# Splitting the gathers of four of the last tiles between GpSimd and two hardware queues

## The chip, the cores and the metric

The kernel runs on one core of one Trainium2 chip. The metric is the device time in microseconds (us) of an execution. An NT of 1574 tiles of 128 edges, some 41,600 instructions, make up one execution.

## The reference, cut to what matters

A relational graph convolution with a residual, over 12,500 nodes of 256 features, 212,500 edges sorted by their target node, and 8 types of edges:

```
h   = max(layernorm(x), 0)
hx  = einsum('ni,rio->rno', h, weight)          # 8 relations
msg = hx[edge_type, src]                        # one row of 256 for each edge
agg = segment_sum(msg, dst, 12500)
out = x + agg * sqrt(0.5) + h_bias + (h @ loop_weight) * sqrt(0.5)
```

The kernel turns the order round: it first sums the normalized rows h[src] by (target, type), and multiplies the sums by the 8 weights afterwards.

## The kernel before, in words

**Tiles and units.** The edges are cut into 1574 tiles (NT) of 128 edges. Two tiles (PAIR) make a unit. For each tile the 128 rows h[src] of 1 KB stand in SBUF, one row a partition, in half of a buffer `msg`; there are 33 such buffers of two tiles. h32 is the normalized table in DRAM.

**Sums.** `edge_sums(t)` multiplies the tile's rows by a one-hot matrix (`oh`, made on VectorE) of its targets and types: four fp32 matmuls on TensorE (L1105), into a PSUM bank `ps`. `add_sums` (L1141, VectorE) adds a unit's sums to the accumulator `acc`, a ring over 768 nodes. When all edges of a group of 128 nodes are summed, 16 products with the weights and 2 with the loop's weight follow (L1321, 32 and 4 matmuls as the profile counts them), VectorE adds x and the bias (L1307, L1338), and SP's queue stores the rows (L1350, and L1341 and L1344 for the last groups). The products of one group are spread between the sums of later tiles. The last group's products can only come after the last tile. Where the ring has turned, `wrap` (L1287) moves its overlap before the next group's products.

**Two ways for a tile's rows.** Most tiles are gathered by one indirect DMA that GpSimd issues (`gather`, L1009). `goal(t)` says how far the gathers run ahead of the sums: 24 tiles in the middle, and `max(8, (NT - t) // 5)` near the end, so 8 tiles in the last 40. Each gather is also held until the last whole unit before its place in the program has been summed ("no faster than the sums"). Its landing is counted on one of 68 semaphores, on which the tile's first matmul waits.

Some tiles (t % 54 in 25 or 53, up to 16 tiles before the end, and also NT - 15 = 1559 and NT - 1 = 1573) are not gathered at all. `begin_fetch(t)` is called 40 tiles (FAR) ahead; it gives the tile its buffer, if it has none yet, and puts five parts (`SOURCES`) on two lists, one for SP's queue (28 + 32 rows) and one for ScalarE's (24 + 20 + 24 rows). From 8 tiles (HOLD) after that, `fetch(n)` takes up to n entries a tile from each list. An entry is either a load of a part's offsets into registers (`load_sources`, L1030) or the DMA of one row (`fetch_row`, L1038). The queues' engines work their instructions off in order and run ahead of the sums as far as buffers and counters permit. SP's queue also carries the loads of x and h (L1258) and the stores of the output; a store waits on VectorE. ScalarE's queue carries little else.

**Counters.** The rows of a fetched tile are counted on one of COUNTERS semaphores, 16 for each row; TensorE waits for the count (L1101) ahead of the tile's matmuls. A semaphore is used again by the fetched tile COUNTERS places later in the list, whose first row waits until the earlier tile is summed.

The fetched tiles near the end are 1483, 1511, 1537, 1559 and 1573.

Of the kernel before, what the change touches and what calls it, by code (L numbers as in the profile page):

```python
# [20 lines left out]
SP = mybir.EngineType.SP  # L21
ACT = mybir.EngineType.Activation

P = 128
# [16 lines left out]
NEAR = 8  # L41
# [21 lines left out]
SINGLE = 54  # L63
PLACED = (25, 53)
CLOSING = 15
SOONER = 64
FETCH = 4
SOURCES = ((0, 28, "SP"), (28, 24, "ACT"), (52, 20, "ACT"), (72, 32, "SP"), (104, 24, "ACT"))
HOLD = 8
FAR = 40  # L70
STORE = 44
COUNTERS = 4
LANDINGS = 68


# [186 lines left out]
def kernel(  # L262
# [11 lines left out]
    nc = tc.nc  # L274
# [10 lines left out]
    NT = plan.NT  # L285
# [46 lines left out]
    def reach_of(t):  # L332
        b, half, row = place_of(t)
        return REACH[half] if b < NB - 1 or NB > 1 and row < NARROWED else (0, WIN)

    def place_of(t):
        u, i = divmod(t, PAIR)
        half = 0 if PAIR * u + 1 == NT else PAIR - 1 - i
        b, row = row_of(u)
        return b, half, row  # L340


    with ExitStack() as main:
# [32 lines left out]
        single, fetches, stores = {}, {SP: [], ACT: []}, []  # L376
        counters = [tc.alloc_semaphore(f"rows{i}") for i in range(COUNTERS)]
        fetched, summed = {}, {}
        landings = [tc.alloc_semaphore(f"landed{i}") for i in range(LANDINGS)]
        landed = {}  # L380
        state = {"h32": None}
# [482 lines left out]
        for d in range(0, N, XG * P):  # L864
            k = min(XG, (N - d) // P)
# [96 lines left out]
        def room(t):  # L962

            both = msgs.tile([P, PAIR, D], F32, name="msg")
            for i in range(PAIR):
                msg[t + i] = both[:, i, :]

        def in_turn(t):

            return t % SINGLE in PLACED  # L970

        def filled(t):

            _, half, _ = place_of(t)
            return min(P, EU - half * P) if t // PAIR == NU - 1 and NB > 1 else P

        def single_rows(t):

            return ((t in (NT - 1, NT - CLOSING) or in_turn(t) and t + 2 * NEAR < NT)
                    and state["h32"] is not None and t // QUAD * QUAD >= state["h32"] + LATE + AHEAD)  # L980

        def begin_fetch(t):

            if t not in msg:
                room(t - t % PAIR)
            fetched[t] = len(fetched)
            for r, n, name in SOURCES:
                engine = SP if name == "SP" else ACT
                fetches[engine].append((
                    done["tile"] + HOLD,  # L990
                    lambda r=r, n=n, engine=engine: load_sources(t, r, n, engine)))

        def gather(t):
            if t % PAIR == 0 and t not in msg:
                room(t)
            if t % QUAD:
                kind[t] = kind[t - 1]
            else:
                kind[t] = "h" if state["h32"] is not None and t >= state["h32"] + LATE else "x"
            table = {"h": h32, "x": x}[kind[t]]  # L1000
            b, i, u = place_of(t)
            if single_rows(t) and t not in fetched and t - done["tile"] >= FAR:
                begin_fetch(t)
            if t in fetched:
                return
            at = i * P + u
            n = filled(t)
            of = direct[:, i : i + 1] if t < PAIR else gidx[b][:, at : at + 1]
            i = nc.gpsimd.indirect_dma_start(  # L1009
                out=msg[t][:n], out_offset=None, in_=table[:, :],  # L1010
                in_offset=bass.IndirectOffsetOnAxis(ap=of[:n], axis=0))
            if kind[t] == "h":
                n = landed[t] = len(landed)
                i.then_inc(landings[n % LANDINGS], 16)
                tc.no_tile_sem_insts.add(i.ins.name)
                tc.add_to_no_dep_group(f"landed{t}", i.ins)
            if "unit" in latest:
                tc.add_manual_dep(
                    i.ins, latest["unit"], SYNC_DEP, reason="no faster than the sums")
# [7 lines left out]
        def load_sources(t, r0, count, engine):  # L1027

            b, _, u = place_of(t)
            _, vals = nc.values_load_multi_w_load_instructions(  # L1030
                single[b][u : u + 1, r0 : r0 + count], engines=[engine],
                min_val=0, max_val=(N - 1) * D * 4,
                skip_runtime_bounds_check_because="clamped to the table where they are computed")
            queue = {SP: nc.sync, ACT: nc.scalar}[engine]
            k = fetched[t]

            def fetch_row(i, v):
                j = queue.dma_start(  # L1038
                    msg[t][r0 + i : r0 + i + 1, :].bitcast(U8), h32_bytes[:, bass.ds(v, D * 4)])
                j.then_inc(counters[k % COUNTERS], 16)  # L1040
                tc.no_tile_sem_insts.add(j.ins.name)
                tc.add_to_no_dep_group(f"rows{t}", j.ins)
                if i == 0 and k >= COUNTERS:
                    tc.add_manual_dep(
                        j.ins, summed[k - COUNTERS], SYNC_DEP, reason="counter is at rest")

            for i, v in reversed(list(enumerate(vals))):
                fetches[engine].insert(0, (0, lambda i=i, v=v: fetch_row(i, v)))

        def fetch(n):  # L1050
            for list_ in fetches.values():
                for _ in range(n):
                    if list_ and list_[0][0] <= done["tile"]:
                        list_.pop(0)[1]()
# [29 lines left out]
        def edge_sums(t):  # L1084
            m, o = msg.pop(t), oh.pop(t)
            if t % PAIR == 0:
                bank = banks[t // PAIR % BANKS]
                sums["ps"] = bank[:, : KC * R * WIN].rearrange("p (c k) -> p c k", c=KC)
            ps = sums["ps"]
            i = t % PAIR  # L1090
            b, half, _ = place_of(t)
            first, width = (R * n for n in reach_of(t))
            end = t == NT - 1 or i == PAIR - 1
            free = added.get(t // PAIR - BANKS)
            if i == 0 and free is not None and latest["pe"] is not None:
                tc.add_manual_dep(latest["pe"], free.name, SYNC_DEP, reason="bank is free")
            if i == 0 and latest["pe"] is not None:
                tc.add_manual_dep(latest["pe"], made[t], SYNC_DEP, reason="one-hots are made")
            if t in fetched:
                k = fetched[t]  # L1100
                j = nc.tensor.wait_ge(counters[k % COUNTERS], 16 * P * (k // COUNTERS + 1))  # L1101
                tc.declare_fence(j.ins, group=f"rows{t}")
            used = filled(t)
            for c in range(KC):
                j = nc.tensor.matmul(  # L1105
                    ps[:, c, first : first + width], m[:used, c * P : (c + 1) * P], o[:used, :width],
                    start=(i == 0 and c == 0), stop=(end and c == KC - 1), skip_group_check=True)
                if t in landed and c == 0:
                    n = landed[t]
                    j.wait_op(landings[n % LANDINGS], 16 * (n // LANDINGS + 1), "sem-ge")  # L1110
                    tc.declare_no_dep(
                        j.ins, group=f"landed{t}", reason="waits for the landing by count")
                    tc.declare_fence(j.ins, group=f"landed{t}")
                else:
                    in_run("sums", j, end and (c == KC - 1 or t == NT - 1))
            latest["pe"] = j.ins
            if end:
                latest["unit"] = j.ins.name
            if t in fetched:
                summed[fetched[t]] = j.ins.name  # L1120
            return ps
# [270 lines left out]
        with tc.manual_schedule():  # L1392
# [21 lines left out]
            for t in range(PAIR):  # L1414
                gather(t)
# [72 lines left out]
            def blocks_ahead(t):  # L1488
                for b in range(1, NB):
                    if b == NB - 1 > 1 and t == PAIR * (RAW + P * (b - 1)) - PREP - SOONER:  # L1490
                        fill_in(b)
# [51 lines left out]
            for t in range(NT):  # L1543
# [5 lines left out]
                    gathered += 1  # L1549
                while t < NT - HELD and stores and stores[0][0] <= t:  # L1550
                    stores.pop(0)[1]()
                fetch(FETCH)
                blocks_ahead(t)
                credit = min(0.0, credit) + SHARE - (0.52 if t % PAIR else 0.0)
                for f in after:
# [27 lines left out]
                if t % (PAIR * REGS) == 0 and t // PAIR + REGS < NU:  # L1583
                    load_offsets(t // PAIR + REGS)
                ps = edge_sums(t)
                while late and late[0][0] <= t:
                    late.pop(0)[1]()
                    credit -= 0.83
                advance(t)
                while writes and credit > 0:  # L1590
                    _, cost, f = writes.pop(0)
# [83 lines left out]
```

## Time and profile before

| what | value |
| --- | --- |
| median of 3 runs | 1936.13 us |
| the three runs | 1936.13, 1936.15, 1932.9 us |
| the profiled execution, its own time | 1932.58 us |
| its span, first to last instruction | 1930.9 us |
| mean granted TensorE clock | 0.960 |
| busy: TensorE matmul, weight load | 1684.4 us (87%), 1441.3 us (75%) |
| busy: VectorE, ScalarE, GpSimd | 1325.9 us (69%), 132.0 us (7%), 1445.7 us (75%) |
| DMA, mean rate | 144 GB/s |

All numbers but the first two rows come from the one profiled execution. PE is TensorE's matmuls, PEld its weight loads, DVE is VectorE, POOL GpSimd; SPq and ACTq are the two hardware queues' issuing instructions, which are not counted as busy. A row of the chain has its start, its length and what it was, in us; a row of the timeline has start, length, engine, line, operation, the tile written and read, the count, and in brackets the engine's idle time before it with what ended it. L1009 is line 1009 of the kernel before.

### The profile page before, as it was taken

To read this page: it belongs to the slowest core of one execution; us is meant where nothing else is said; L and a number is where in the kernel's file an instruction comes from. 1 tells how busy PE (TensorE), PEld (TensorE's weight loads), DVE (VectorE), ACT (ScalarE), POOL (GpSimd) and SP (SyncE) were. 2 spreads that over 40 slices of the span, in tenths; PEclk is the share of its full clock that TensorE was granted. 3 is DMA by queue.
4 is the path that set the end of the run, shared out by engine and by line. 5 is a ranking of instruction groups with operands and counts; after the bars stand their busy time and mean duration, and the time that the engine had idled before them with its cause. 6 is when DMAs were issued, how large, how long until landed. Compare 5 with 4: busy or idle time off the path is not lost.

```text
span 1930.9 us, 41561 instructions
## 1 busy us (share of the span) xinstructions
PE 1684.4 (87%) x10136; PEld 1441.3 (75%) x10136; DVE 1325.9 (69%) x3353; ACT 132.0 (7%) x286; POOL 1445.7 (75%) x1546
## 2 busy tenths in 40 slices
PE   2367999999889999989888989898989888999998
PEld 2356889899778777777777777777777777777887
DVE  7888768976567965658766656776566885665653
ACT  6964000000000000000000000000000000000000
POOL 7777777777777777777777777777777777777774
PEclk9568999999999999999999999999999999999999
DMA  9974455445544444454444454444445444444443
GB/s 322 382 222 146 121 141 142 142 132 141 145 126 140 123 131 138 126 144 130 132 131 121 136 139 131 130 130 132 131 128 142 122 130 132 132 127 132 128 109 88
DMA packets 159057, 278.88 MB, mean 144 GB/s; under 512 B 35819, under 2 KB 110168, under 8 KB 158808
## 3 DMA queue, kind: packets, MB, share of 16 engines
q0 software_dynamic: 72960, 199.33, 36.3%
q1 hardware_dynamic: 77000, 73.08, 12.3%
q10 hardware_dynamic: 8848, 3.78, 1.0%
q8 instruction: 80, 1.31, 0.3%
q14 instruction: 169, 1.38, 0.2%
HBM read 250.45 MB, written 25.60 MB: 143 GB/s over the span
## 4 chain that ended last, share of the span: by engine, by line
PE 31%; POOL 27%; DMA 20%; issue 11%; DVE 7%; ACT 3%; DVEq 0%; SPq 0%; POOLq 0%; ACTq 0%
POOL msg L1009 27%; DMA msg<-h,gidx 19%; PE po L1321 16%; PE ps L1105 15%; ACT msg L931 1%; DVE acc L1141 1%; DVE stats L887 1%; DMA xt<-in_x_dram 1%; DVE oh L1066 1%; DVE moves L478 1%; ACT xt L931 1%; DVE acc L1183 1%; PE pt L1165 1%; ACT acc L1154 0%; DVE fixed L480 0%
## 5 line engine op out<-in xcount | busy, mean ns | idle before, releaser
L1009 POOL DMA_INDIRECT msg<-h,gidx x1432 | 1360.2, 950 | 439.1 <-issue 375.9
L1105 PEld LDWEIGHTS ps<-oh,msg 128*128 128x128 f32 x6296 | 915.7, 196 | 384.7 <-DMA msg<-h,gidx 261.9
L1105 PE MATMUL ps<-oh,msg 128*128 128x136 f32 (+1 forms) x6296 | 998.9, 288 | 197.6 <-DMA msg<-h,gidx 131.5
L1321 PE MATMUL po<-w,acc 128*128 128x256 f32 (+1 forms) x3136 | 881.5, 386 | 4.2 <-DVE acc L1141 3.0
L1141 DVE TENSOR_TENSOR acc<-acc,ps 128x352 f32 x788 | 406.5, 516 | 363.0 <-PE ps L1105 351.3
L1321 PEld LDWEIGHTS po<-w,acc 128*128 128x128 f32 (+1 forms) x3136 | 515.3, 192 | 42.0 <-issue 11.3
L1183 DVE SCALAR_TENSOR_TENSOR acc<-types,pt 128x256 f32<-128x256 bf16 x720 | 258.9, 412 | 76.0 <-PE pt L1165 65.3
L1066 DVE TENSOR_TENSOR oh<-fixed,cols 128x544 f32<-128x544 f32 x394 | 281.4, 714 | 0.0
L1321 PE MATMUL po<-wl,self_t 128*128 128x256 f32 (+1 forms) x392 | 111.8, 409 | 5.4 <-DVE self_t L1170 4.6
L1009 POOL DMA_INDIRECT msg<-in_x_dram,gidx x86 | 81.5, 948 | 26.2 <-issue 23.5
L1321 PEld LDWEIGHTS po<-wl,self_t 128*128 128x128 f32 (+1 forms) x392 | 71.2, 203 | 13.5 <-DVE self_t L1170 5.9
L1307 DVE TENSOR_TENSOR xr<-xr,po 128x256 f32<-128x256 f32 (+1 forms) x98 | 40.5, 413 | 19.1 <-PE po L1321 19.0
L1338 DVE TENSOR_TENSOR xr<-xr,po 128x256 f32<-128x256 f32 (+1 forms) x98 | 41.2, 421 | 10.4 <-PE po L1321 7.0
L478 DVE TENSOR_SCALAR moves<-fixed 128x336 int32<-128x336 int32 (+1 forms) x96 | 44.6, 465 | 5.2 <-DVE acc L1141 3.7
L931 ACT ACTIVATE msg<-msg,shift,rstd 128x256 f32<-128x256 f32 x88 | 44.8, 587 | 6.9 <-DVE stats L895 4.5
L480 DVE COPY_PREDICATED fixed<-moves,fixed 128x335 int32<-128x335 int32 (+7 forms) x96 | 41.6, 433 | 3.3
L1237 DVE CAST types<-pt 128x512 bf16<-128x512 f32 x23 | 15.9, 690 | 40.0 <-PE pt L1233 39.1
L1170 DVE COPY self_t<-pt 128x256 f32<-128x256 f32 (+1 forms) x98 | 40.6, 414 | 2.2 <-PE pt L1165 2.2
L1165 PE MATMUL pt<-ident,hr 128*128 128x128 f32 (+1 forms) x196 | 38.3, 278 | 2.9 <-DMA hr<-h 1.5
L931 ACT ACTIVATE xt<-xt,shift,rstd 128x256 f32<-128x256 f32 x66 | 33.7, 587 | 9.8 <-DVE shift L928 9.8
L1221 DVE TENSOR_TENSOR of<-pt,line 22x512 bf16<-22x512 f32 x23 | 15.7, 682 | 20.4 <-PE pt L1214 20.2
L1165 PEld LDWEIGHTS pt<-ident,hr 128*128 128x128 f32 (+1 forms) x196 | 25.3, 149 | 5.3 <-DMA hr<-h 1.8
(179 smaller groups left out, 373.8 us busy)
## 6 DMA issues: line engine op xcount, KB each, us to landing
msg<-h ACTq DMA_DIRECT2D x3672, 1.0 KB
msg<-h SPq DMA_DIRECT2D x3240, 1.0 KB
msg<-h,gidx POOLq DMA_INDIRECT x1432, 5.1
hr<-h SPq DMA_DIRECT2D x23, 512.0 KB
xr<-in_x_dram SPq DMA_DIRECT2D x23, 512.0 KB
out_dram<-xr SPq DMA_DIRECT2D x22, 512.0 KB
xt<-in_x_dram SPq DMA_DIRECT2D x16, 512.0 KB
h<-xt SPq DMA_DIRECT2D x16, 512.0 KB
```

Of the source, the lines that this page charges most:

```text
L478: nc.vector.tensor_single_scalar(m, packed[:, :n], 1 << (bit + k), op=ALU.bitwise_and)
L480: nc.vector.copy_predicated(packed[:, : n - (1 << k)], m[:, 1 << k :], packed[:, 1 << k : n])
L931: nc.scalar.activation(row, row, AF.Relu, bias=shift[:n, j : j + 1], scale=rstd[:n, j : j + 1])
L1009: i = nc.gpsimd.indirect_dma_start(out=msg[t][:n], out_offset=None, in_=table[:, :], in_offset=bass.IndirectOffsetOnAxis(ap=of[:n], axis=0))
L1066: j = nc.vector.tensor_tensor(o[:, k : k + v, :i, :width], iota_f[:, :width].unsqueeze(1).unsqueeze(1).to_broadcast([P, v, i, width]), of. ...
L1105: j = nc.tensor.matmul(ps[:, c, first : first + width], m[:used, c * P : (c + 1) * P], o[:used, :width], start=(i == 0 and c == 0), stop=( ...
L1141: i = nc.vector.tensor_tensor(a, a, ps[:, c], op=ALU.add)
L1165: in_run("turns", nc.tensor.transpose(pst[:, c, :n], rows_[:n, c * P : (c + 1) * P], ident[:n, :n]), c == KC - 1)
L1170: nc.vector.tensor_copy(got["self", g][:, :, :n], pst[:, :, :n])
L1183: i = nc.vector.scalar_tensor_tensor(acc[:, :, r, s0 : s0 + n], of, float(r + 1), pst[:, :, :n], op0=ALU.is_equal, op1=ALU.mult)
L1321: i = nc.tensor.matmul(got["out", g][:n], lhs, rhs, start=(r == R and c == 0), stop=(r == R - 1 and c == KC - 1))
L1338: nc.vector.tensor_add(rows_[:n, k, :], rows_[:n, k, :], got["out", g][:n])
```

## The change

Four more of the last tiles are treated in both ways at once. `SPLIT` gives, by their distance from NT, how many of their 128 rows GpSimd still gathers, and which rows the two queues fetch one by one:

| tile | GpSimd | SP | ScalarE's queue |
| --- | --- | --- | --- |
| 1565 (NT - 9) | 124 | 4 | 0 |
| 1567 (NT - 7) | 96 | 16 | 16 |
| 1569 (NT - 5) | 92 | 16 | 20 |
| 1571 (NT - 3) | 64 | 32 | 32 |

TensorE waits for both counts at these tiles: for the gather's landing and for the rows' counter. The counters become eight, and each keeps the sum of the rows counted on it so far, as the tiles now differ in their numbers. In the last 40 tiles `fetch` takes up to 8 entries a tile from each list, not 4. The pairs 1564 to 1570 get their buffers 40 tiles ahead, with the fetched rows.

```
+SPLIT = {
+    9: (124, ((124, 4, "SP"),)),
+    7: (96, ((96, 16, "SP"), (112, 16, "ACT"))),
+    5: (92, ((92, 16, "SP"), (108, 20, "ACT"))),
+    3: (64, ((64, 32, "SP"), (96, 32, "ACT"))),
+}
...
-COUNTERS = 4
+COUNTERS = 8
...
+        counted = [0] * COUNTERS
...
         def single_rows(t):
-            return ((t in (NT - 1, NT - CLOSING) or in_turn(t) and t + 2 * NEAR < NT)
+            return ((t in (NT - 1, NT - CLOSING) or NT - t in SPLIT or in_turn(t) and t + 2 * NEAR < NT)
...
         def begin_fetch(t):
-            for r, n, name in SOURCES:
+            for r, n, name in SPLIT.get(NT - t, (0, SOURCES))[1]:
...
         def gather(t):
-            if t in fetched:
-                return
             at = i * P + u
             n = filled(t)
+            if t in fetched:
+                n = SPLIT.get(NT - t, (0, SOURCES))[0]
+            if not n:
+                return
...
         def edge_sums(t):
             if t in fetched:
-                k = fetched[t]
-                j = nc.tensor.wait_ge(counters[k % COUNTERS], 16 * P * (k // COUNTERS + 1))
+                k = fetched[t] % COUNTERS
+                counted[k] += 16 * sum(n for _, n, _ in SPLIT.get(NT - t, (0, SOURCES))[1])
+                j = nc.tensor.wait_ge(counters[k], counted[k])
...
-                fetch(FETCH)
+                fetch(FETCH if t < NT - FAR else 2 * FETCH)
```

## The prediction

> **What bounds the kernel now.** I read the page first (the chain's shares, the costliest group), then the chain of waits piece by piece through the last 90 us, then the queues' own issues in time, then single rows of TensorE and GpSimd. Tile numbers come from counting back along both engines: the last gather is tile 1572 and a gather is 1.25 us (0.95 busy, 0.30 between), so the gather at 1885.85 us is tile 1550's; four fp32 matmuls on L1105 are one tile's sums.
>
> ```profile
> POOL msg L1009 27%; DMA msg<-h,gidx 19%; PE po L1321 16%; PE ps L1105 15%; ACT msg L931 1%; DVE acc L1141 1%; DVE stats L887 1%; DMA xt<-in_x_dram 1%; DVE oh L1066 1%; DVE moves L478 1%; ACT xt L931 1%; DVE acc L1183 1%; PE pt L1165 1%; ACT acc L1154 0%; DVE fixed L480 0%
> L1009 POOL DMA_INDIRECT msg<-h,gidx x1432 | 1360.2, 950 | 439.1 <-issue 375.9
> ```
>
> GpSimd's gathers set the pace of the whole span, and the time in which a gather's rows are on their way (19%) is the second share. The end looks otherwise, in the chain's pieces (start, length, what):
>
> ```profile
> 1845.83 6.46 DMA msg<-h,gidx
> 1852.29 0.04 issue
> 1852.33 3.66 PE ps L1105 x16
> ...
> 1885.85 2.74 DMA msg<-h,gidx
> 1888.58 0.04 issue
> 1888.63 0.73 PE ps L1105 x4
> ...
> 1900.85 2.76 DMA msg<-h,gidx
> ...
> 1905.51 1.56 PE po L1321 x6
> ...
> 1917.95 7.19 PE po L1321 x32
> ```
>
> Two things are to be seen. The last wait for a gather on this chain ends at 1903.6, 2.76 us after 1900.85: tile 1563. All four tiles whose gathers the change shortens (1565, 1567, 1569, 1571) come after it, and from 1905.51 on TensorE works without waiting for any gather. And a gather took 6.46 us to land at 1845.83, 2.74 and 2.76 at 1885.85 and 1900.85. What differs is seen in the issues of the two queues (start, length of the stretch, count):
>
> ```profile
> 1774.23 26.71 SPq L1038 DMA_DIRECT2D msg<-h  x66
> ...
> 1803.53 17.06 SPq L1038 DMA_DIRECT2D msg<-h  x46
> 1829.49 0.41 SPq L1350 DMA_DIRECT2D out_dram<-xr  x1
> 1830.00 29.14 SPq L1038 DMA_DIRECT2D msg<-h  x74
> 1839.80 26.18 ACTq L1038 DMA_DIRECT2D msg<-h  x68
> L1030 ACTq TENSOR_LOAD <-single x17: 1536/1791/2713, 1700.1 to 1855.9; - x17
> L1030 SPq TENSOR_LOAD <-single x11: 1829/2124/2226, 1702.2 to 1846.6; - x11
> ```
>
> At 1845 both queues fetch single rows; the last row of tile 1573 is issued at 1859.1 on SP and at 1866.0 on ScalarE's queue, and after that gathers land in 2.7 us. More of it, from the chain earlier on, and from one wait that TensorE's row shows (tile 1488, gathered at 1810.81, awaited until 1818.03, so 7.2 us):
>
> ```profile
> 482.79 12.25 DMA msg<-h,gidx
> ...
> 1780.78 5.21 DMA msg<-h,gidx
> 1794.54 5.83 DMA msg<-h,gidx
> 1810.81 0.95 POOL L1009 DMA_INDIRECT msg<-h,gidx  x1 [0.30 <-issue]
> 1818.03 0.73 PE L1105 MATMUL ps<-oh,msg 128*128 128x136 f32 x4 [0.61 <-DMA msg<-h,gidx]
> ```
>
> With both queues at it from 1774 to 1820 the landing grows: 5.2, 5.8, 7.2 us. Then SP stands still for 8.9 us (1820.6 to 1829.5, the output store waits), and at 1845.8 it is 6.5. So fetched rows delay gathers, more the longer both queues run, and the last 40 us are the one stretch that is free of them. The change puts 136 more rows there.
>
> ```profile
> q10 hardware_dynamic: 8848, 3.78, 1.0%
> msg<-h ACTq DMA_DIRECT2D x3672, 1.0 KB
> ```
>
> ScalarE's queue moves 3672 rows of 1 KB in at most 8848 packets, about two for a row (the row and its completion): a row isn't spread over the 16 DMA engines. That one engine gets them all is not in these rows. [...]
>
> **The change part by part.**
>
> *Shorter gathers.* 4 + 32 + 36 + 64 = 136 rows leave GpSimd. In proportion that is 136/128 of 0.95 us, 1.0 us; at a fixed price of an instruction it is 0. Nothing shorter than 128 rows is in the trace, so 0 to 1.0. Either way it is hidden:
>
> ```profile
> 1903.35 0.95 POOL L1009 DMA_INDIRECT msg<-h,gidx  x1 [0.30 <-issue]
> 1912.10 0.95 POOL L1009 DMA_INDIRECT msg<-h,gidx  x1 [0.30 <-issue]
> 1908.67 0.59 PE L1105 MATMUL ps<-oh,msg 128*128 128x104 f32 x4
> 1914.80 2.71 PE L1105 MATMUL ps<-oh,msg 128*128 128x104 f32 x20
> L1101 PEldq EVENT_SEMAPHORE  x54: 51/51/51, 264.0 to 1914.9; - x54
> ```
>
> Tile 1565 lands about 1906.1 and is used at 1908.67; tile 1572 lands at 1914.85 and its matmuls, thirteenth of the last 20, come about 1.3 us later. I take 0.
>
> *Four more counter waits on TensorE*, 51 ns each, 0.2 us, on the queue that loads weights ahead. Between 0 and 0.2 I take 0.1.
>
> *Eight counters for four.* The first row of a fetched tile waits until the tile k places earlier in the list is summed. With four, tile 1573 would now wait for 1565, which is summed at 1908.67, too late; with eight it waits for tile 1483, ninety tiles earlier, of which GpSimd gathers 86 at 1.25 us: some 107 us before 1916.7. 0, and 0 for the earlier ones, which now wait for a sum further back.
>
> *Rows on ScalarE's queue.* 16 + 20 + 32 = 68 rows and 3 loads of offsets, ahead of tile 1573's 68 rows and 3 loads. The same set took 26.2 us plus its first load, 28 us, so tile 1573's last row goes out at 1866 + 28 = 1894 instead of 1866.
>
> *Rows on SP.* 4 + 16 + 16 + 32 = 68 rows and 4 loads. From tile 1534 on up to eight entries a tile are put on a queue, so the output store at 1829.49 now has behind it not 46 of tile 1559's 60 rows but all of them, tile 1565's four, and two loads: 18 rows at 0.32 us (17.06 less one load, over 46) and 2 loads of 2.2 are 10.2 us from 1820.6. The idle 8.9 us are filled and the store goes at 1830.8, 1.3 us later; nothing waits for it. Then 124 rows and 4 loads, 40 + 9 us, end at 1880 instead of 1859. Tile 1573 is summed from 1916.7: 22 us to spare on the slower queue.
>
> *What these rows do to the gathers.* Both queues now run unbroken from 1774 to 1880, then one until 1894. No row has the landing at 1885.85 (tile 1550, on the chain) under this load. Below: 2.74, if one queue alone does no harm, or 6.46, the value after 16 us of both. Above: 12.25, the value that the early part shows. From 7.2 at 1811 with the growth of 2.0 us in 30 us it would be about 11.8 at 1880; it then falls while ScalarE's queue is alone. I take 8. That is 5.3 us later than 2.74. TensorE takes some back:
>
> ```profile
> 1902.41 0.73 PE L1105 MATMUL ps<-oh,msg 128*128 128x136 f32 x4 [0.30 <-DMA msg<-h,gidx]
> 1903.65 0.69 PE L1105 MATMUL ps<-oh,msg 128*128 128x104 f32 x4 [0.51 <-DMA msg<-h,gidx]
> 1880.97 1.50 PE L1105 MATMUL ps<-oh,msg 128*128 128x104 f32 x12
> 1883.34 0.95 POOL L1009 DMA_INDIRECT msg<-h,gidx  x1 [0.30 <-issue]
> ```
>
> After 1888.63 it idles 0.30 + 0.51 = 0.81 us before the ring's wrap on VectorE ends and the next products start at 1905.51; afterwards only the last group's hand-over is idle, which moves along. So 5.3 - 0.8 = 4.5 us reach the end. A second effect adds: a gather is also held behind the sums of nine tiles before it. Tile 1548's (1883.34) waits for tile 1539's sums (first of the twelve matmuls from 1880.97, done 1881.55): 1.8 us to spare. TensorE has no idle time between 1852.33 and 1878, so a lateness of about 2 us from longer landings at 1852 arrives there whole and holds GpSimd by some 0.2 us, which no later gather makes up; at 3 us it would be 1.2. I take 0.4.
>
> *Sum:* 0 + 0.1 + 0 + 4.5 + 0.4 = 5.0 us. The profiled execution took 1932.58 us (span 1930.9), so 1937.6 against it. It is 3.6 us below the median of the runs shown, two of which are at 1936.1 and one at 1932.9; against the median it is 1936.13 + 5.0 = 1941.
>
> **The rivals.**
>
> *The landings recover in time.* Below 7.4 us at 1885.85 (2.74 + 0.81 + 3.9) less than 3.9 us reach the end, 0.2%, about what a measurement of this kernel can tell from no change. 6.46 gives 2.9 us: 1939. For it speaks that SP fills its rows with loads of 2.1 us, one for every 16 rows; against it that 7.2 was reached before the pause that now goes.
>
> *Rows and gathers don't collide there* (rows spread, or the growth had another cause): then TensorE's own work decides from 1905.51, and the time is 1936.2, not slower. It decides if the landing at 1885.85 stays under 3.6 us. Against it stand 6.46 and 2.74 on the two sides of the last fetched row.
>
> *GpSimd is the bound to the end*, and 136 rows less bring up to 1.0 us: 1935. Against it: 1.3 us to spare at tile 1572. More than 1.0 us isn't in it, so faster by over 0.2% needs the spread of the runs as well.
>
> *An uneven gather lands late.* 124 and 92 rows don't divide into 16 equal shares. If such a gather landed over 2.6 us later (tile 1565, 1908.67 - 1906.1) TensorE would stall at it; twice 2.7 us of landing would cost 0.1 us. [...]
>
> *The rows come too late for tile 1573*: it needs a pitch near twice 0.32 us. 1945 or more.
>
> **How the numbers follow.** Forecast (4 us and more) 0.57, late rows 0.03: slower 0.60. Recovery in time 0.24, no collision 0.09: the same 0.33. Faster 0.07, GpSimd's rows with a low run. Range: from the lower group of runs with little added (1932.6 + 1.4 = 1934) to a landing of 12 us and a GpSimd hold of 3 (1936.1 + 8.5 + 3 = 1948). The forecast's own range is 1937 to 1948.
>
> **What would show it.** Right: rows of L1038 on ScalarE's queue until about 1894 and on SP until 1880, no pause before the store on L1350; landings of 6 us and more on the chain between 1866 and 1885; longer waits on L1105 for gathers there; GpSimd's gaps over 0.30 us around tile 1548. The last stretch from 1905.51 to the end of the last group's products at 1925.14 keeps its 19.6 us. Wrong: landings near 2.8 us at 1885 with rows still being issued, or a gap before tile 1565's, 1569's or 1573's sums.

## The result, and the profile after

The changed kernel takes 1939.76 us (median of 8 runs, 1938.61 to 1942.82), the kernel before 1933.42 us (8 runs, 1931.02 to 1936.15): a ratio of 1.0032, 95% interval 1.0021 to 1.0043, so 6.3 us slower. All runs named e, f and h below were timed while the chip ran even the kernel before in 2387 to 2414 us, at a granted clock of 0.88 to 0.90 instead of 0.96, so every ratio is taken against the kernel before as timed beside that run. The profiled execution took 1940.04 us with a span of 1938.3 us, 7.4 us more than the one before. The lines of the changed kernel are shifted: the gather is L1018, the row fetch L1047, the sums L1115, their counter wait L1111, the products L1331, the wrap L1297.

The chain of the changed kernel, its last 75 us (start, length, what):

```profile
1867.02 9.98 DMA msg<-h,gidx
1877.00 0.04 issue
1877.04 1.18 PE ps L1115 x8
...
1891.18 0.08 issue
1891.26 5.75 DMA msg<-h,gidx
1897.01 0.04 issue
1897.05 0.73 PE ps L1115 x4
...
1912.76 1.56 PE po L1331 x6
...
1925.19 7.19 PE po L1331 x32
```

A gather took 9.98 us to land at 1867.02; in the kernel before, the last row had gone out by then (1866.0). The last gather on the chain is the same tile's as in the prediction's argument, 1550 (the 22nd from the end, the last one counted): it begins at 1891.26 instead of 1885.85 and lands in 5.75 us instead of 2.74. From 1897.05 no gather is waited for. The products after the wrap begin 7.25 us later than before (1912.76 against 1905.51), the last group's 7.24 us later (1925.19 against 1917.95): the tail itself is unchanged, it only starts late.

The queues' issues in time:

```profile
1804.14 23.93 SPq L1047 DMA_DIRECT2D msg<-h  x64
1830.13 0.41 SPq L1360 DMA_DIRECT2D out_dram<-xr  x1
1830.72 49.60 SPq L1047 DMA_DIRECT2D msg<-h  x124
1760.05 135.62 ACTq L1047 DMA_DIRECT2D msg<-h  x324
```

SP puts out all 60 rows of tile 1559 and four more ahead of the store, without the pause, and ends at 1880.3; ScalarE's queue ends at 1895.7.

GpSimd's gathers with a gap over 0.35 us, and the four short ones (1908.77, 1911.64, 1914.13, 1916.88) with the last:

```profile
1870.49 0.94 POOL L1018 DMA_INDIRECT msg<-h,gidx  x1 [1.27 <-PE pt L1175]
...
1875.59 0.94 POOL L1018 DMA_INDIRECT msg<-h,gidx  x1 [0.40 <-PE ps L1115]
...
1880.89 0.94 POOL L1018 DMA_INDIRECT msg<-h,gidx  x1 [0.61 <-PE ps L1115]
...
1885.26 0.94 POOL L1018 DMA_INDIRECT msg<-h,gidx  x1 [2.17 <-PE ps L1115]
...
1888.76 0.95 POOL L1018 DMA_INDIRECT msg<-h,gidx  x1 [1.31 <-PE ps L1115]
...
1908.77 1.30 POOL L1018 DMA_INDIRECT msg<-h,gidx  x1 [0.30 <-issue]
...
1911.64 0.92 POOL L1018 DMA_INDIRECT msg<-h,gidx  x1 [0.30 <-issue]
...
1914.13 1.19 POOL L1018 DMA_INDIRECT msg<-h,gidx  x1 [0.30 <-issue]
...
1916.88 0.91 POOL L1018 DMA_INDIRECT msg<-h,gidx  x1 [0.31 <-issue]
1918.09 0.95 POOL L1018 DMA_INDIRECT msg<-h,gidx  x1 [0.30 <-issue]
```

Before, none of the gaps in this stretch was over 0.31 us. Over that pace the five add 0.97 + 0.10 + 0.31 + 1.87 + 1.01 = 4.3 us, each ended by TensorE: GpSimd was held behind the sums. The rest of the 5.4 us by which tile 1550's gather begins late was there before any of the added rows went out. The gather that is 80th from the end, in the profile before and in this one:

```profile
1813.31 0.95 POOL L1009 DMA_INDIRECT msg<-h,gidx  x1 [0.30 <-issue]
...
1814.46 0.95 POOL L1018 DMA_INDIRECT msg<-h,gidx  x1 [0.30 <-issue]
```

It begins 1.15 us later, and so does every gather from there to 1867 (1.15 to 1.18 us). So of the 7.25 us by which the products after the wrap begin late, 6.1 arose after 1867; the medians differ by 6.3.

TensorE in turn waits for gathers:

```profile
1874.62 0.69 PE L1115 MATMUL ps<-oh,msg 128*128 128x104 f32 x4 [0.99 <-DMA msg<-h,gidx]
1876.13 0.73 PE L1115 MATMUL ps<-oh,msg 128*128 128x136 f32 x4 [0.81 <-DMA msg<-h,gidx]
...
1892.06 0.69 PE L1115 MATMUL ps<-oh,msg 128*128 128x104 f32 x4 [0.31 <-DMA msg<-h,gidx]
1893.87 1.16 PE L1115 MATMUL ps<-oh,msg 128*128 128x136 f32 x8 [1.11 <-DMA msg<-h,gidx]
1895.36 1.45 PE L1115 MATMUL ps<-oh,msg 128*128 128x136 f32 x8 [0.34 <-DMA msg<-h,gidx]
1897.05 0.73 PE L1115 MATMUL ps<-oh,msg 128*128 128x136 f32 x4 [0.24 <-DMA msg<-h,gidx]
```

### The profile page after: what moved, and what is told of

The parts are those of the page before. It is cut to its first block, busy times and chain, and to the rows that moved or that the text cites. A ratio compares the mean times of both kernels' runs of the same rounds, so it can differ in the third digit from the quotient of the medians.

```text
span 1938.3 us, 41854 instructions
## 1 busy us (share of the span) xinstructions
PE 1686.6 (87%) x10136; PEld 1441.7 (74%) x10136; DVE 1326.8 (68%) x3353; ACT 132.0 (7%) x286; POOL 1447.9 (75%) x1546
## 4 chain that ended last, share of the span: by engine, by line
PE 35%; POOL 24%; DMA 21%; issue 10%; DVE 7%; ACT 3%; SPq 0%; DVEq 0%; POOLq 0%; ACTq 0%
POOL msg L1018 24%; DMA msg<-h,gidx 19%; PE po L1331 17%; PE ps L1115 16%; DVE acc L1151 1%; ACT msg L938 1%; DVE stats L894 1%; DVE acc L1193 1%; DVE oh L1075 1%; DMA xt<-in_x_dram 1%; DVE moves L485 1%; PE pt L1175 1%; DMA xr<-in_x_dram 1%; PE pt L1224 0%; DMA h<-xt 0%
## 5 line engine op out<-in xcount | busy, mean ns | idle before, releaser
L1018 POOL DMA_INDIRECT msg<-h,gidx x1432 | 1362.5, 951 | 442.8 <-issue 376.8
L1115 PEld LDWEIGHTS ps<-oh,msg 128*128 128x128 f32 x6296 | 916.0, 196 | 389.2 <-DMA msg<-h,gidx 266.4
L1115 PE MATMUL ps<-oh,msg 128*128 128x136 f32 (+1 forms) x6296 | 1000.7, 288 | 200.7 <-DMA msg<-h,gidx 134.2
L1331 PE MATMUL po<-w,acc 128*128 128x256 f32 (+1 forms) x3136 | 884.6, 387 | 4.3 <-DVE acc L1151 3.0
L1331 PEld LDWEIGHTS po<-w,acc 128*128 128x128 f32 (+1 forms) x3136 | 517.3, 193 | 42.6 <-issue 10.8
L1331 PE MATMUL po<-wl,self_t 128*128 128x256 f32 (+1 forms) x392 | 109.4, 402 | 7.4 <-DVE self_t L1180 5.8
L1018 POOL DMA_INDIRECT msg<-in_x_dram,gidx x86 | 81.4, 946 | 26.2 <-issue 23.2
L1331 PEld LDWEIGHTS po<-wl,self_t 128*128 128x128 f32 (+1 forms) x392 | 69.8, 199 | 15.6 <-DVE self_t L1180 7.0
L1317 DVE TENSOR_TENSOR xr<-xr,po 128x256 f32<-128x256 f32 (+1 forms) x98 | 40.7, 415 | 19.6 <-PE po L1331 19.6
L1231 DVE TENSOR_TENSOR of<-pt,line 22x512 bf16<-22x512 f32 x23 | 15.7, 682 | 21.4 <-PE pt L1224 21.2
```

Source lines behind the costliest of these rows:

```text
L1018: i = nc.gpsimd.indirect_dma_start(out=msg[t][:n], out_offset=None, in_=table[:, :], in_offset=bass.IndirectOffsetOnAxis(ap=of[:n], axis=0))
L1115: j = nc.tensor.matmul(ps[:, c, first : first + width], m[:used, c * P : (c + 1) * P], o[:used, :width], start=(i == 0 and c == 0), stop=( ...
L1331: i = nc.tensor.matmul(got["out", g][:n], lhs, rhs, start=(r == R and c == 0), stop=(r == R - 1 and c == KC - 1))
```

## The experiments

**At the pace of the first profiles: g1, half the bytes.** The 136 rows are fetched in number, but with half their length; the other rows of the last tiles, those of 1573 among them, keep their 1 KB.

```
+                bytes_ = D * 2 if NT - t in SPLIT else D * 4
                 j = queue.dma_start(
-                    msg[t][r0 + i : r0 + i + 1, :].bitcast(U8), h32_bytes[:, bass.ds(v, D * 4)])
+                    msg[t][r0 + i : r0 + i + 1, : bytes_ // 4].bitcast(U8), h32_bytes[:, bass.ds(v, bytes_)])
...
             for c in range(KC):
+                if c and NT - t in SPLIT:
+                    used = SPLIT[NT - t][0]
```

> The changed kernel with the 136 rows of the four split tiles fetched as 512 B instead of 1 KB; the second half of their features is summed over GpSimd's rows alone, so 136 half rows are left out. Theory (what counts is how many row fetches there are, not their bytes): as the changed kernel, 1.003 of before and landings of 9 to 11 us near 1875 where rows go out every 0.32 us; 1.010 to 1.015 with tile 1573's rows late by some 18 us where they go out every 0.7 us. Rival (bytes): half of the loss in both, 1.0015 and 1.006, and landings near 6 us.

Measured: 1940.52 us against 1933.72, a ratio of 1.0035 (1.0021 to 1.0049). The landings on its chain, and two of GpSimd's holds:

```profile
1851.89 8.94 DMA msg<-h,gidx
...
1873.44 9.79 DMA msg<-h,gidx
...
1892.10 5.88 DMA msg<-h,gidx
...
1873.44 0.95 POOL L1018 DMA_INDIRECT msg<-h,gidx  x1 [2.56 <-PE pt L1178]
1888.60 0.94 POOL L1018 DMA_INDIRECT msg<-h,gidx  x1 [2.17 <-PE ps L1118]
```

The half rows are on their way on SP's queue from 1834 to 1864 us and on ScalarE's from 1847 to 1876, by the packets of this trace; the rows behind them are tile 1573's, at full length. So of these landings the first is the one to compare: 8.94 us at 1851.89, with half rows on both queues, where the changed kernel's gathers at 1850.75 and 1853.25 landed after 8.68 and 9.18 (by the landing counts in its trace). The later two, 9.79 and 5.88 us against 9.98 and 5.75, come mostly under whole rows. With the time unchanged as well, nothing is gained from half the bytes, and the rival of the bytes is out: what counts here is the number of row fetches. The packets agree: between 1840 and 1860 us a row's data took 46 ns in the changed kernel and a half row's 27 ns in g1 (medians), out of some 320 ns from one row of a queue to the next. What else a row costs is not shown.

**At the same pace: g2, no rows at all.** The kernel before, with every tile gathered by GpSimd.

```
-            return ((t in (NT - 1, NT - CLOSING) or in_turn(t) and t + 2 * NEAR < NT)
+            return (False
```

> The kernel before without any tile fetched row by row: GpSimd gathers all 1574 tiles. Theory: where rows go out every 0.32 us, gathers land in 2.7 to 2.8 us everywhere, GpSimd's 54 gathers more at 1.25 us cost 55 to 70 us, 1.03 of before. On the chip of the last two calls TensorE's and the queues' instructions come one every 0.7 us in places, GpSimd is busy for 61% only: there 6912 row fetches with their register moves fall away, and if they are what starves TensorE's issue, the time falls to 2000 to 2250 us (0.84 to 0.94 of before). Rival (TensorE's slow issue on that chip has nothing to do with the row fetches): 0.98 to 1.02.

Measured: 1998.51 us against 1933.72, 1.0338 (1.0321 to 1.0355): 64.8 us for 54 gathers more, 1.20 us each, close to GpSimd's 1.25. From its page, the busy line and the chain's shares, and the landings on its chain:

```profile
PE 1720.6 (86%) x10136; PEld 1447.4 (72%) x10136; DVE 1327.8 (67%) x3353; ACT 132.0 (7%) x286; POOL 1495.8 (75%) x1600
...
1885.46 3.10 DMA msg<-h,gidx
1891.70 2.74 DMA msg<-h,gidx
1911.70 2.72 DMA msg<-h,gidx
1929.18 2.78 DMA msg<-h,gidx
1949.18 4.11 DMA msg<-h,gidx
```

Without rows gathers land in 2.7 to 4.1 us on the chain. Over the span from 400 us the median landing is 2.8 us against 4.7 in the kernel before, the longest 6.8 against 12.2; so "2.7 to 2.8 us everywhere" was too strict. The fetched rows are what makes gathers late, and they are worth it over the whole kernel, by the 64.8 us. What g2 takes at the slower pace wasn't tried.

**At the slower pace: the other ten.** There TensorE and the queues get out one instruction every 0.7 us in stretches. The row in the waits' list of the changed kernel (f1) for TensorE's idle time that nothing shown ended (in the first profile of the same kernel it is 0.8 us, once), and SP's row fetches in the chain of e3:

```profile
PE ps L1115 <- issue: 223.4, 315, 3.8
...
2355.07 0.70 SPq L1047
2355.79 0.70 SPq L1047
...
2357.23 0.23 SPq L1047
2357.55 0.23 SPq L1047
```

GpSimd is busy for 60% of this span (75% at the first pace), so gathers don't set the pace here. What makes the chip so slow isn't known. The runs still tell which part of the change costs, but by another mechanism. Five runs have all 136 rows more:

f1 is the changed kernel itself.

> The changed kernel once more, beside the next three on one chip. On the chip of the first four experiments a queue got out a row only every 0.7 us, and there 136 rows more cost 1.4%, with a shorter fetch limit as well as with earlier gathers. Theory: where rows go out every 0.32 us as in the first profiles, 1.003 of before (1.002 to 1.005), through late landings and GpSimd's holds; where they go out every 0.7 us, 1.012 to 1.016, through tile 1573's rows that come too late. Rival (the split does no harm by itself, the first timing was chance): 1.000.

e3 has `fetch(... FETCH + 1)` instead of `2 * FETCH`, so up to five entries a tile.

> The changed kernel, but up to five entries a tile from each list in the last 40 tiles instead of eight; the same 136 rows more, the output store on SP comes after fewer of them, so most of SP's pause stays. Theory (number of rows in the last stretch counts, the pause eases it): SP's rows end near 1887 us, landings at 1866 to 1885 of 5 to 7 us, time +2 to +5 us over before, most likely +3.5. Rival (order alone): 0 to +1 us, since the pause is back.

e4, f3 and h2 are one kernel, the changed one with an earlier gather near the end:

```
-CLOSE = 8
+CLOSE = 14
```

> The changed kernel with CLOSE = 14: near the end a gather is placed 14 tiles ahead of the sums instead of 8, so it is held behind earlier sums. Theory: GpSimd's gaps over 0.30 us between 1866 and 1890 (1.27, 0.61, 2.17, 1.31 us in the changed kernel) go, its last gather starts near 1912 instead of 1918 us; the landings stay long while rows are fetched (7 us or more at 1885), so part of the loss stays: +2 to +5 us over before, most likely +3.5, that is 3 us less than the changed kernel. Rival (the landings alone set the end, the hold is only a consequence): within 1 us of the changed kernel, +5.5 to +7.

> As e4_close14: the changed kernel with gathers placed 14 tiles ahead at the end. Theory: with rows every 0.32 us GpSimd's gaps over 0.30 us after 1866 go, and the time is 2 to 5 us over before, 1 to 4 us under f1. With rows every 0.7 us no change against f1. Rival (hold is only a consequence): as f1 in both.

> The changed kernel with gathers placed 14 tiles ahead of the sums near the end, not 8. Where GpSimd paces the span: theory (GpSimd's hold, 4 to 6 us, is part of the loss): its gaps over 0.35 us after 1866 go, tile 1550's gather starts near 1886 instead of 1891, still lands in 6 us or more, and the time is +2 to +5 us over before, against +6.3 to +6.8 of the changed kernel. Rival (the long landings alone set the end, the hold only follows): +5.5 to +7. Where instructions come one every 0.7 us: 1.01 to 1.015 as before.

Five have none of these rows more, or nearly so. e1 and f2 are the changed kernel with `SPLIT = {}`: the fetch limit and the counters alone.

> The changed kernel without the split tiles: no row more, no gather shorter, but eight counters and up to eight entries a tile from each list in the last 40 tiles. Theory (the 136 added rows crowd the gathers' landings): SP's pause before the output store is filled, its rows end near 1850 us and ScalarE's queue's at 1866 as before; from 1869 on gathers land in 2.8 us again. Time 0 to 3.5 us over before, most likely +1.5. Rival (order alone: it is the filled pause on SP, not the number of rows): +5 us or more, near the changed kernel's +6.3.

> As e1_fetch_only: eight entries a tile and eight counters, no split tiles. Theory: with rows every 0.32 us +0 to +3.5 us (0.998 to 1.002 of before), its landings back at 2.8 us from 1869 on; with rows every 0.7 us no change. Rival (order alone): as f1.

e2 is the kernel before with the shorter gathers alone:

```
+SHORT = {9: 124, 7: 96, 5: 92, 3: 64}
...
-            n = filled(t)
+            n = SHORT.get(NT - t, filled(t))
...
-            used = filled(t)
+            used = SHORT.get(NT - t, filled(t))
```

> The kernel before with the shorter gathers alone: GpSimd gathers 124, 96, 92 and 64 rows of the four tiles, nobody fetches the others, and the matmuls of these tiles sum only the gathered rows (136 rows are left out of the sums). Theory: the same time as before within 1 us, since TensorE doesn't wait for a gather after 1905 us; gathers of 124 and 92 rows take 1.3 and 1.2 us as in the changed kernel, those of 96 and 64 rows 0.9. Rival (the uneven gathers at the end cost the time): +3 us or more. A third view (GpSimd's rows bound the end): -1 us.

h1 is e1 and e2 together, everything of the change but the rows.

> The changed kernel without the 136 fetched rows: GpSimd gathers 124, 96, 92 and 64 rows of the four tiles, eight counters, up to eight entries a tile from each list, but nobody fetches the rest (136 rows are left out of the sums). Where GpSimd paces the span, as in the first profiles: theory (the rows are the cause): landings of 2.8 us from 1872 on, GpSimd's last gather within 1.5 us of the one before (1912.1), time -0.5 to +2.5 us over before, most likely +1, for SP's filled pause. Rival (order or uneven gathers): +5 us or more. Where instructions come one every 0.7 us: no change, 0.998 to 1.002.

f4 is the changed kernel with `t == NT - CLOSING` for `t in (NT - 1, NT - CLOSING)`: GpSimd gathers the last tile, and 128 fetched rows fall away.

> The changed kernel, but the last tile (1573) is gathered by GpSimd, so 128 rows leave the queues: in all 8 rows more than before, in another place. Theory (the number of rows in the last stretch counts): rows end near 1866 us, gathers land in 2.8 us from 1870 on, time within 1.5 us of before; with rows every 0.7 us also as before, 0.998 to 1.003. Rival (splitting tiles and waiting for two counters costs by itself): as f1.

| run | rows more than before | ratio, 95% interval | TensorE's waits for row counters in the last 70 us: longest, all |
| --- | --- | --- | --- |
| f1 changed kernel | 136 | 1.0124 (1.0078 to 1.0171) | 18.6, 18.6 us |
| e3 five entries | 136 | 1.0137 (1.0103 to 1.0170) | 21.5, 29.6 us |
| e4 CLOSE 14 | 136 | 1.0142 (1.0116 to 1.0168) | 21.5, 30.0 us |
| f3 CLOSE 14 | 136 | 1.0128 (1.0081 to 1.0175) | 21.4, 30.6 us |
| h2 CLOSE 14 | 136 | 1.0141 (1.0110 to 1.0172) | 21.4, 40.6 us |
| e1 limit and counters | 0 | 0.9997 (0.9980 to 1.0015) | none |
| f2 the same | 0 | 1.0003 (0.9976 to 1.0030) | 8.3, 8.9 us |
| e2 short gathers | 0 | 0.9996 (0.9977 to 1.0014) | 4.3, 7.8 us |
| h1 all but the rows | 0 | 1.0008 (0.9988 to 1.0028) | 5.5, 5.5 us |
| f4 last tile gathered | 8 | 1.0018 (0.9992 to 1.0043) | 8.8, 8.8 us |

The rows cost the 1.2 to 1.4% there; without them neither the rest of the change (h1) nor the splitting itself (f4) shows a cost clear of its interval. Where the rows cost it are TensorE's waits for row counters, all at tile 1573 in f1, at an earlier tile too in the other four. In the order of the table the profiled executions of the five took 16.0, 28.0, 33.2, 32.5 and 43.5 us more than the median of the kernel before, near the sums of the waits. That is agreement and no proof: the five single executions without the rows lie 9.0 us below to 19.6 above, and the kernel before has no trace at this pace. The row of TensorE at tile 1573 and the queues' last stretch in f1, and TensorE's row in h1:

```profile
2341.48 41.27 SPq L1047 DMA_DIRECT2D msg<-h  x92
2339.94 3.49 ACTq L1047 DMA_DIRECT2D msg<-h  x11
2383.97 1.54 PE L1115 MATMUL ps<-oh,msg 128*128 128x176 f32 x4 [18.61 <-PEq L1111]
...
2393.62 1.54 PE L1111 MATMUL ps<-oh,msg 128*128 128x176 f32 x4 [5.47 <-PEq L1107]
```

SP is still fetching rows 39 us after ScalarE's queue has ended, and the last tile waits 18.6 us for them. That is the prediction's rival of rows that come too late, which takes a pitch near twice 0.32 us: here it is 0.7 in places. The expectations of e1 to e4 were written for the first pace. At this one they are untested, though e1 and e2 came out near theirs; e3 and e4 (2 to 5 us) missed by far, at some 30 us, through the late rows. Those of the f and h runs had a part for this pace, and it held in all six; what f3 and h2 were to show of GpSimd's hold stays untested.

## Why the prediction was right

The forecast of 1941 us stands against 1939.76, and 5.0 us more against 6.3. The place and the mechanism are those of the forecast; two terms of the sum were mis-sized and made up for each other, which is luck. The base was lucky too: 1936.13 us, the median of three runs, stands 2.7 us above the median of eight (1933.42), so the forecast is 1.2 us above the measured time although its sum is 1.3 us too small.

*The rows crowd the gathers: right.* On the chain 9.98 us at 1867.02 was measured, where 6 and more were to be seen until 1885; at 1891.26 it was 5.75. g2 shows 2.7 to 4.1 us without rows, g1 that the number of rows counts and not their bytes. Where the growth comes from is seen in the landing counts of the trace: at 1891.26 fifteen of the gather's sixteen are in by 2.7 us, and one comes at 5.75; at 1867.02 fifteen by 2.8, and one at 9.98. So one of 16 counts is late. A row is one packet of 1024 B in the trace (3740 of them on ScalarE's queue, for its 3740 rows), with one of 4 B after it. That every row holds up the same one of a gather's sixteen counts would fit this, but it isn't shown: on which DMA engine a packet ran isn't in the trace, and whether rows spread over more engines would ease it wasn't tried. The 8 us of the sum don't rest on it: they were estimated from the landings before (5.2 to 7.2 us, and 12.25).

*The ends of the queues: right.* 1880 and 1894 us were forecast, 1880.3 and 1895.7 measured. The store on SP went at 1830.13 without a pause (1830.8).

*The landing's term: too high.* I took 8 us for tile 1550's gather and 4.5 us at the end. It was 5.75, so 3.0 us more than before instead of 5.3: this gather began 5.4 us later than before, and by then SP's rows had ended 11 us ago. For the time at which I had it begin, 1885.85, the 8 us was well chosen: by the landing counts the gathers at 1885.26 and 1886.51 took 8.56 and 7.51 us. What was wrong is when it would begin.

*GpSimd's hold: far too low.* I took 0.4 us; the five gaps hold 4.3. I had put TensorE's lateness at 1881 at 2 us, from landings a little over the 6.46 of before, but they had grown to 8.7 by 1850.75 and 9.98 by 1867, and TensorE's waits of 0.99 and 0.81 us at 1874 to 1876 came on top. With 1.8 us to spare, further lateness went into GpSimd's schedule, and none of it was made up by the last gather. Together: 5.4 us later begun (4.3 of hold, the rest there before the rows) and 3.0 later landed make 8.4 at TensorE (1888.63 to 1897.05); 7.25 reach the products after the wrap, so 1.2 us were taken back, 0.8 in the forecast. How much of the loss would remain if GpSimd weren't held, the kernel with CLOSE = 14 was to show; it ran only at the slower pace, so the split into landing and hold is read from the profile and not shown by a run.

*Shorter gathers: hidden, but priced on the wrong side.* I allowed 0 to 1.0 us saved. They took 1.30, 0.92, 1.19 and 0.91 us against 0.95 each: 0.5 us more. TensorE's last stretch doesn't notice, as forecast (7.19 us for the last group, no wait for a gather), and e2 and h1 agree at the slower pace.

*Counter waits and counters:* nothing to be seen; the stretch from the products after the wrap to the last product takes 19.6 us in both.

*The rivals.* Recovery in time didn't come about at 1550, though at 5.75 the landing was under its 7.4 us: its condition left out the hold. No collision and GpSimd as the bound to the end are refuted by the profile after. The uneven gather is real and harmless: the 124-row gather landed after 4.59 us, the 92-row one after 3.93, the former with twelve counts at 2.6 us and four from 4.3 on. Tile 1565's spare time (2.6 us before) covered it.

*What stays open.* How the loss at the first pace divides between the filled pause on SP and the 136 rows: e1, f2 and h1, which have the order without the rows, ran only at the slower pace, where no cost of it shows (1.0008 at most, the interval up to 1.0030). At the first pace both are always present. The landing counts of the two profiles bear on it: gathers begun between 1840 and 1860 us took 7.4 to 9.2 us against 5.1 to 7.2 before, and both can have a part in that. Those begun between 1868 and 1883 took 8.9 to 10.9 against 2.7 to 4.0. Before, all rows were out at 1866.0, and another order of the same rows on SP wouldn't make ScalarE's queue end later; so this second part, with most of the hold, is put down to the added rows. That is argued from the profile, not shown by a run.

## What to carry to other kernels

Row fetches that were issued ahead "for free" made the transfers late that the critical engine waits for: gathers begun between 1868 and 1883 us landed in 8.9 to 10.9 us with rows in flight, in 2.7 to 4.0 without. What the two share wasn't shown. Look at the landing times on the chain with and without them in flight, not at the DMA share (0.4 here). Taking work off an engine pays only ahead of the last wait on it: here all four relieved gathers (1908.77 us and later) came after that wait (until 1897.01), while the rows that replaced them ran before it. When a producer is held behind its consumer (a short lead near the end), a late landing can be paid twice, once as itself (here 3.0 us) and once as a hold (4.3 us, of which the producer made up nothing).

## What the runs showed of the hardware that was not expected

An indirect gather of 124 rows keeps GpSimd 1.30 us and one of 92 rows 1.19, while 128 take 0.95, 96 take 0.92 and 64 take 0.91: fewer rows saved next to nothing, and the two counts that aren't multiples of 16 cost 0.25 to 0.35 us more, and 1.2 to 1.9 us of landing (3.93 us with 92 rows and 4.59 with 124, against 2.7). A gather landed some 9 us after its start while two queues fetched single rows at a pitch of 0.32 us each, with 512 B a row (8.94 us) as with 1 KB (8.68 and 9.18 us), and only one of its sixteen landing counts was late.
